# Layer 1's last group of a four-layer graph network: row sums ended pair by pair, and the gate of three pairs written in one row on TensorE

## The chip, the cores and the metric

The kernel runs on one core of one Trainium2 chip, in float32 throughout. The metric is the device time of one execution in microseconds (us); the median of several runs counts. One execution was also taken by the hardware profiler; all times inside the kernel are from it and are counted from the start of its span.

## The reference

There are N = 2708 rows of D = 256 values and one dense matrix `adj` (2708 x 2708). Four layers follow one another; each has a graph part and a feed-forward part, and both are added to x. The change lies in layer 1:

```python
# graph part
A = adj + eye;  D = 1 / sqrt(sum(A, axis=1));  A = A * D[:, None] * D[None, :]
x = x + relu(A @ (layernorm(x) @ W) + b)
# feed-forward part: one of 8 experts for each row, by its gate
H      = gelu(layernorm(x) @ W1 + b1)             # 256 -> 1024, the same W1 for all
probs  = softmax(H @ Wg + bg);  assign = argmax(probs)
x      = x + probs[assign] * (H @ Wd[assign] + bd[assign])
```

## The kernel before

**Tiles and groups.** The rows are cut into 22 tiles of 128 (the last has 20 rows). In layer 1 they are worked off in three groups, tiles 0 to 7, 8 to 15 and 16 to 21 (`GROUPS1`). A group's graph part is a loop over the 22 row blocks j of `adj`: SyncE loads the row block `adrow` (four buffers), VectorE makes a mask of it (L1165) and adds the identity where the block meets the group's own rows (L1168), and TensorE adds one product for each of the group's tiles (L1196) into PSUM banks `acc2` that hold two tiles each, a pair. After the last j, `grow` (L1147, L1149) adds the sums to x on VectorE. In the last group the pairs are tiles 16 and 17, tiles 18 and 19, and tile 20 with the 20 last rows (tile 21, whose sums come earlier from `last_sums`).

**The gate, `send1`.** For a group it takes mean and variance of the rows (`stats`, with an inverse root of eleven short VectorE instructions), and then goes pair by pair: normalise (L187), turn on TensorE (`turn_to`, L203), copy on ScalarE (L204), the products with W1 into eight blocks of 128 hidden values (`hidden`, L357) with Gelu on ScalarE (L359), the gate's products (L1092), a copy (L1095), their addition over four quarters (L1099, L1100). H itself is transposed on VectorE (L1109, into two buffers `hrow`) and stored in device memory as `hid`, by ScalarE's queue in the last group and by GpSimd's in the others (L1115, L1118). Then come softmax, the choice of an expert and `route` (L384, L386 on TensorE), which gives each row its place in a list ordered by expert; GpSimd scatters each row's name and weight there (`taken`, L495).

**The blocks, `Units`.** The second product goes in blocks of 128 rows of one expert. For each block GpSimd gathers the names (L509), then the rows of `hid` into one of three buffers `hs` (L649); TensorE turns them (L660, eight transposes) and ScalarE copies them into one of three buffers `hTs` (L661); SyncE loads the expert's weights `wb` of 1,152 KB (L1032, three buffers); TensorE multiplies (L699, into one of two PSUM banks `yacc`); VectorE adds the bias and multiplies by the weight (`ys`, L700, L701); GpSimd scatters the result (`given`, L495). Blocks 0 to 8 (`NA` = 9) hold rows of the first two groups only, so that they can run before the last group is routed; blocks 9 to 23 need that routing. After the last scatter layer 2 loads `given` (`mine`, L56).

**What sets the order.** Each engine works off its own list in the order in which it stands. The framework's planner makes that list from the order of the source, its own costs and the dependences; `add_manual_dep` with `NoSync` fixes the order of two instructions in it, with no semaphore. Loads, stores, gathers and scatters stand in the lists of the engines that issue them (SyncE, ScalarE, GpSimd), and a waiting one holds up those behind it. In the kernel before, blocks 0 to 8 come after `send1` in the source, and the planner mixes the two.

Of the kernel before, what the change touches and what calls it, by code (L numbers as in the profile page):

```python
# [8 lines left out]
F32 = mybir.dt.float32  # L9
# [57 lines left out]
def adj_ffn4(ctx: ExitStack, tc: tile.TileContext, a: dict, out: bass.AP):  # L67
# [79 lines left out]
    def after(i, past):  # L147

        tc.add_manual_dep(i.ins, past, mybir.DependencyInfo(
            mybir.DependencyClass.NoSync, mybir.DependencyReason.DATA), reason="order")  # L150

    def rsqrt(pool, val, n):
# [467 lines left out]
    class Units(Blocks):  # L620
# [58 lines left out]

        def run(self, pool, items, during=None):  # L680
            self.names_todo += items
            self.todo += items
            self.rows_todo += len(items)
            self.more()
            turned = self.turn(pool, self.rows[0][1])
            n = 0
            while self.rows:
                w2, hT = self.ahead.pop(0), turned
                m, _ = self.rows.pop(0)
                self.more()  # L690
                if during is not None:
                    during(n)
                n += 1
                if self.rows:
                    turned = self.turn(pool, self.rows[0][1])
                y = pool.tile([P, D], F32, name="ys", bufs=2)
                q = pools["psum"].tile([P, W], F32, name="yacc", bufs=2)[:, :D]
                for f in range(HC):
                    te.matmul(q, lhsT=hT[:, f, :], rhs=w2[:, f, :], start=(f == 0), stop=(f == HC - 1))  # L699
                v.tensor_tensor(y, q, w2[:, HC, :], ALU.add)  # L700
                v.tensor_scalar(y, y, m[:, 1:2], None, op0=ALU.mult)  # L701
                scatter(self.given, m[:, 0:1].bitcast(I32), y, self.given.shape[0] - 1, self.ok)

    def count_left(pool, *what):
# [317 lines left out]
    with ExitStack() as l1:  # L1022
# [47 lines left out]

        def send1(tiles):

            G = len(tiles)
            t0 = tiles[0]
            st = stats(tiles)
            names = gt.tile([P, GM, 2], F32, name="names", bufs=1)[:, :G]
            lg = gt.tile([P, G, E], F32, name="lg", tag=f"lg{G}")
            v.memset(lg[:, G - 1, :], 0.0)
            for i0 in range(0, G, 2):
                own = [(i, (i - i0) * P, rows(tiles[i])) for i in range(i0, min(i0 + 2, G))]  # L1080
                w = own[-1][1] + own[-1][2]
                xT = gt.tile([P, DC, 2 * P], F32, name="xT4", bufs=2)
                for i, k, r in own:
                    xn = work.tile([P, D], F32, name="xn")[:r]
                    norm_to(xn, tiles[i], i, st)
                    turn_to(xT[:, :, k : k + r], xn, r)
                hT = gt.tile([P, HC, 2 * P], F32, name="hT", bufs=1)
                hidden(hT, xT, w1, lambda f: b1[:, f : f + 1], 0, w, HC)
                p = ps_tmp()
                for f in range(HC):  # L1090
                    q = f % 4 * Q
                    te.matmul(p[q : q + Q, :w], lhsT=wg[:, f, :], rhs=hT[:, f, :w],  # L1092
                              start=(f < 4), stop=(f >= HC - 4), tile_position=(0, q))
                lT = gt.tile([P, 2 * P], F32, name="lT", bufs=1)
                s.copy(lT[:, :w], p[:, :w])  # L1095
                p = ps_tmp()
                for i, k, r in own:
                    o = p[:r, (i - i0) * E : (i - i0 + 1) * E]
                    te.matmul(o, lhsT=lT[:, k : k + r], rhs=fold[:, :E], start=True, stop=True)  # L1099
                    v.tensor_tensor(lg[:r, i, :], o, bg[:r], ALU.add)  # L1100

                queue = s if tiles is GROUPS1[-1] else g
                for i, k, r in own:
                    h = gt.tile([P, P // Q, HC * Q], F32, name="hrow", bufs=2)
                    n = -(-r // Q)
                    if r < P:
                        v.memset(hT[:, :, k + r : k + n * Q], 0.0)
                    for f in range(0, HC, 4):
                        v.transpose(h[:, :n, f * Q : (f + 4) * Q].rearrange("p b (f i) -> p f b i", i=Q),  # L1109
                                    hT[:, f : f + 4, k : k + n * Q].rearrange(  # L1110
                                        "p f (b j) -> p f b j", j=Q))
                    for q in range(P // Q):
                        dst = hid[tiles[i] * P : tiles[i] * P + r, q * HC * Q : (q + 1) * HC * Q]
                        if r == P:
                            queue.dma_start(dst.rearrange("(b j) c -> j b c", j=Q),  # L1115
                                            h[q * Q : (q + 1) * Q])
                        else:
                            queue.dma_start(dst, h[q * Q : q * Q + r, 0, :])  # L1118
            pin()
            probs = softmax8(gt, lg, G)  # L1120
            sel, best = first_max(gt, probs, G)
            g.tensor_copy(names[:, :, 0:1].bitcast(I32), choice1[:, t0 : t0 + G, :])
            v.tensor_copy(names[:, :, 1:2], best)
            ix = route(gt, (sel,), G, t0 * P, rows(tiles[-1]), known)
            for i, t in enumerate(tiles):
                r = rows(t)
                scatter(taken[1], ix[:r, i, :], names[:r, i, :], N - 1, "taken1")
# [5 lines left out]
                lambda t, r, p, by: s.activation(sup[:r, t, :], p, AF.Copy, scale=by))  # L1133
        hid = tc.dram_tile([N, HC * P], F32, name="hid")
        work1 = Units(hw, given[1], weights1, hid)
        for tiles in GROUPS1:
# [3 lines left out]
            pairs = banks(tiles)  # L1140
            acc = [gsum.tile([P, 2, D], F32, name="acc2", bufs=4) for _ in pairs]

            def grow(p, t, m, q):
# [8 lines left out]
            for j in [*range(12), FULL, *range(12, FULL)]:  # L1152
# [33 lines left out]
                if j == FULL:  # L1186
                    for n, t, k in by_turns(own):
                        last_product(acc[n // 2][:, n % 2, :], n // 2, ad, k, sup[:, FULL, :],
                                     False)
                    continue  # L1190
                for p, pair in zip(acc, pairs):
                    for n in pair:
                        if n == len(own):
                            continue
                        _, k, q = own[n]
                        te.matmul(p[:q, n - pair[0], :], lhsT=ad[:, k : k + q],  # L1196
                                  rhs=sup[:r, j, :], start=(j == 0 and n == pair[0]),
                                  stop=(j == FULL - 1 and n == pair[-1]))
            for p, pair in zip(acc, pairs):
                if pair[0] < len(own):  # L1200
                    t, m = own[pair[0]][0], len(pair)
                    grow(p[:, :m, :], t, m, P)
            if end:
                sums.close()
# [5 lines left out]
                    tc.tile_pool(name="c1", side="right", reuse_waits="tile", bufs=1))  # L1210
                work1.more()
            send1(tiles)
            if tiles is GROUPS1[-2]:
# [6 lines left out]
        more = [(rest, b, past, taken[1], False) for b in range(ALWAYS, MOST - NA)]  # L1220
        left = []

        def beside(b):
            if b == NA + 4:
                left.append(blocks_left(too_many, MOST))
                as_bc = row_bc(work, "L2_gnn_attn_src", D, "elu_e")
                ad_bc = row_bc(work, "L2_gnn_attn_dst", D, "elu_e")
                g.dma_start(w_l2[:, :, :D], a["L2_gnn_WT"].rearrange("(c p) n -> p c n", p=P))
                score_columns(w_l2, D, as_bc, 1, D)
                score_columns(w_l2, D, ad_bc, 1, D + 1)  # L1230
                centre(w_l2)

        work1.run(hc, items, beside)
        work1.run_rest(hc, more, left[0])

# [19 lines left out]

    def in_order(first, engines):

        was = {}
        for i in nc.cur_bb.bb.instructions[first:]:
            if i.engine in engines:  # L1260
                if i.engine in was:
                    tc.add_manual_dep(i, was[i.engine], mybir.DependencyInfo(
                        mybir.DependencyClass.NoSync, mybir.DependencyReason.DATA), reason="order")
                was[i.engine] = i.name


# [4 lines left out]
    with tc.tile_pool(name="t3", reuse_waits="tile", bufs=1) as t3:  # L1271
# [7 lines left out]
        psum_pool(sums, 3, 5)  # L1279
        tp = t3  # L1280
        wr = mat(tp, "L2_ffn_Wr", E)
        br = row_bc(tp, "L2_ffn_br", E)
# [7 lines left out]
        wa = tp.tile([P, DC, D + 2 * NH], F32, name="w_l3")  # L1290
        g.dma_start(wa[:, :, :D], a["L3_gnn_WT"].rearrange("(c p) n -> p c n", p=P))

        SUMMED = NT - 2
# [633 lines left out]
```

## Time and profile before

| | us |
|---|---|
| median of 3 runs (lowest, highest) | 1924.65 (1923.59, 1931.69) |
| the profiled execution, its own time | 1928.12 |
| its span | 1926.4 |
| TensorE busy | 1825.9 (95%) |
| VectorE, ScalarE, GpSimd busy | 1095.6, 641.6, 342.8 |
| mean granted TensorE clock | 0.979 |

A float32 product is two instructions in the trace, so that the eight products of a block are sixteen. Timeline rows give start, length, engine, line, operation, tiles, count, and in brackets how long the engine stood idle before and what ended that. Line numbers are those of the kernel before.

### The profile page before, as it was taken

How to read it: one execution, taken by the hardware profiler on the slowest of the kernel's cores; microseconds unless marked ns; L12 is line 12 of the kernel's file. 1: busy time of each engine (PE TensorE's matmuls, PEld its weight loads, DVE VectorE, ACT ScalarE, POOL GpSimd, SP SyncE). 2: the span in 40 equal slices, each digit the busy share in tenths (PEclk: the TensorE clock that was granted, in tenths of full speed). 3: DMA queues.
4: the chain of work that ended last, by engine and by line, in shares of the span. 5: the costliest groups of instructions: out<-in, count | busy, mean ns of one | idle time of the engine just before them, and what ended most of it. 6: DMA issues, size and time to landing. Idle time of an engine off the chain costs nothing.

```text
span 1926.4 us, 25726 instructions
## 1 busy us (share of the span) xinstructions
PE 1825.9 (95%) x9453; PEld 1326.4 (69%) x9453; DVE 1095.6 (57%) x2483; ACT 641.6 (33%) x1457; POOL 342.8 (18%) x405
## 2 busy tenths in 40 slices
PE   7999999999998999999787799999899999999998
PEld 6888788888887888887676678888556732232344
DVE  7777872443434443354432265555354398999897
ACT  7868752222223204021222142222242552031131
POOL 1004254333321002213436300000000000000000
PEclk9999999999998999999898899999899999999999
DMA  8435658887764454636777610000101000001000
GB/s 275 138 111 163 215 200 296 317 317 287 269 265 139 125 156 116 152 109 130 227 231 283 252 54 1 1 1 1 44 1 34 17 1 23 23 12 28 20 20 15
DMA packets 90141, 243.94 MB, mean 127 GB/s; under 512 B 18159, under 2 KB 44823, under 8 KB 80792
## 3 DMA queue, kind: packets, MB, share of 16 engines
q1 hardware_dynamic: 70048, 197.09, 31.1%
q0 software_dynamic: 16960, 42.42, 7.0%
q10 hardware_dynamic: 3000, 2.70, 0.5%
q8 instruction: 78, 1.28, 0.3%
q14 instruction: 55, 0.45, 0.1%
HBM read 216.29 MB, written 28.71 MB: 127 GB/s over the span
## 4 chain that ended last, share of the span: by engine, by line
PE 71%; DMA 14%; DVE 6%; issue 4%; ACT 2%; POOL 2%; SPq 0%; POOLq 0%; DVEq 0%; ACTq 0%
PE num L1825 10%; PE ps_acc L1404 9%; PE acc L907 9%; PE acc L1196 8%; PE ps_tmp L357 7%; DMA given<-ys,xs 6%; PE den L1835 5%; PE ps_acc L573 4%; PE ps_tmp L250 4%; PE yacc L607 4%; PE ps_acc L1588 3%; DMA hs<-hid,names 2%; DMA names<-taken,b_ix 1%; DVE e L1795 1%; DMA given<-ys,names 1%
## 5 line engine op out<-in xcount | busy, mean ns | idle before, releaser
L1795 DVE SCALAR_TENSOR_TENSOR e<-arena,G,mask 128x1024 f32<-128x1024 f32 (+1 forms) x264 | 287.0, 1150 | 13.6 <-PE den L1835 13.6
L1825 PE MATMUL num<-e,wh 128*64 128x512 f32 (+4 forms) x1056 | 215.5, 551 | 0.0
L907 PE MATMUL acc<-msg,wt 128*128 128x256 f32 x882 | 200.1, 384 | 1.9 <-DVE x L932 1.9
L1404 PE MATMUL ps_acc<-hh,e 128*128 128x257 f32 x882 | 199.2, 382 | 1.7 <-ACT o L1349 1.7
L1196 PE MATMUL acc<-sup,adrow 128*128 128x256 f32 x882 | 198.6, 381 | 1.5 <-DVE adrow L1168 1.5
L907 PEld LDWEIGHTS acc<-msg,wt 128*128 128x128 f32 x882 | 166.9, 192 | 28.1 <-DVE x L932 2.6
L1196 PEld LDWEIGHTS acc<-sup,adrow 128*128 128x128 f32 x882 | 165.0, 190 | 28.5 <-issue 5.2
L1404 PEld LDWEIGHTS ps_acc<-hh,e 128*128 128x128 f32 x882 | 163.7, 190 | 29.2 <-ACT o L1349 4.3
L573 PE MATMUL ps_acc<-xTs,wa 128*128 128x256 f32 (+1 forms) x768 | 169.4, 373 | 3.0 <-DVE xTs L563 2.9
L607 PE MATMUL yacc<-wb,hTs 128*128 128x256 f32 x736 | 168.3, 380 | 0.0
L575 ACT ACTIVATE hTs<-ps_acc,wa 128x256 f32<-128x256 f32 (+1 forms) x192 | 88.9, 465 | 235.4 <-PE yacc L607 161.2
L573 PEld LDWEIGHTS ps_acc<-xTs,wa 128*128 128x128 f32 x768 | 136.5, 190 | 29.4 <-DVE xTs L563 5.8
L1825 PEld LDWEIGHTS num<-e,wh 128*64 128x64 f32 (+1 forms) x1056 | 66.6, 136 | 126.9 <-issue 106.2
L607 PEld LDWEIGHTS yacc<-wb,hTs 128*128 128x128 f32 x736 | 137.1, 190 | 17.7 <-DVE ys L609 0.2
L1398 DVE SCALAR_TENSOR_TENSOR e<-Rb,G,mask 128x640 f32<-128x640 f32 (+2 forms) x110 | 85.1, 775 | 93.1 <-PE ps_acc L1404 93.0
L1835 PE MATMUL den<-e,wh 128*32 128x512 f32 (+4 forms) x1056 | 118.0, 548 | 0.0
L204 ACT COPY xT<-ps_tmp 128x256 f32<-128x256 f32 x98 | 33.7, 365 | 243.2 <-PE ps_tmp L203 219.5
L1165 DVE TENSOR_SCALAR mask<-adrow 128x1024 uint8<-128x1024 f32 (+1 forms) x66 | 41.7, 631 | 123.4 <-DMA adrow<-in_adjT 123.2
L699 PE MATMUL yacc<-wb,hTs 128*128 128x256 f32 x384 | 91.2, 389 | 0.0
L865 DVE SCALAR_TENSOR_TENSOR wt<-adrow,wt 128x640 f32<-128x640 f32 (+3 forms) x67 | 71.1, 1064 | 28.9 <-ACT wt L141 28.5
L1835 PEld LDWEIGHTS den<-e,wh 128*32 128x32 f32 (+1 forms) x1056 | 30.2, 108 | 77.8 <-issue 73.7
L495 POOL DMA_INDIRECT given<-ys,xs x46 | 65.5, 1424 | 81.0 <-DVE ys L610 68.0
(454 smaller groups left out, 2572.7 us busy)
## 6 DMA issues: line engine op xcount, KB each, us to landing
adhalf<-in_adjT SPq DMA_DIRECT2D x42, 677.0 KB
wb<-in_L_ffn_W2p SPq DMA_DIRECT2D x24, 1152.0 KB
wb<-in_L_ffn_Wdp SPq DMA_DIRECT2D x24, 1152.0 KB
wa<-in_L_ffn_W1b SPq DMA_DIRECT2D x24, 1028.0 KB
adrow<-in_adjT SPq DMA_DIRECT2D x42, 512.0 KB
adrow<-in_adjT SPq DMA_DIRECT2D x42, 320.0 KB
adrow<-in_adjT SPq DMA_DIRECT2D x21, 576.0 KB
adrow<-in_adjT SPq DMA_DIRECT2D x21, 448.0 KB
```

The source lines that it names most:

```text
L357: te.matmul(p[:, :w], lhsT=w1[:, c, f * P : (f + 1) * P], rhs=xnT[:, c, c0 : c0 + w], start=(c == 0), stop=(c == DC - 1))
L573: i = te.matmul(p[:, f % 2, : m * P], lhsT=w1[:, c, f * P : (f + 1) * P], rhs=xT[:, c, : m * P], start=(c == 0), stop=(c == DC - 1))
L575: s.activation(hT[:, f, : m * P], p[:, f % 2, : m * P], AF.Gelu, bias=bias[:, f : f + 1])
L607: te.matmul(q[:, k, :], lhsT=hT[:, f, k * P : (k + 1) * P], rhs=w2[:, f, :], start=(f == 0), stop=(f == HC - 1))
L699: te.matmul(q, lhsT=hT[:, f, :], rhs=w2[:, f, :], start=(f == 0), stop=(f == HC - 1))
L907: te.matmul(p[:q, n - pair[0], :], lhsT=wt[:, k : k + q], rhs=msg[:r, j, :], start=(j == 0 and n == pair[0]), stop=(j == FULL - 1 and n == ...
L1196: te.matmul(p[:q, n - pair[0], :], lhsT=ad[:, k : k + q], rhs=sup[:r, j, :], start=(j == 0 and n == pair[0]), stop=(j == FULL - 1 and n == ...
L1398: v.scalar_tensor_tensor(e[:r, :w], Rb[:r, c0 : c0 + w], G[:r, j, :], mask[:r, j, c0 : c0 + w], op0=ALU.max, op1=ALU.mult)
L1404: te.matmul(p[:, : D + 1], lhsT=e[:, k : k + q], rhs=hh[:, j, :], start=(j == 0), stop=False)
L1795: v.scalar_tensor_tensor(e[:, :w], slow[:, m % 2, k, :w], G[:, j, 2 * pair + k, :], mask[:, j, c0 : c0 + w], op0=ALU.max, op1=ALU.mult)
L1825: te.matmul(num[k * DK : (k + 1) * DK, hf, :q], lhsT=wh[some, j, 2 * pair + k, :DK], rhs=e[some, h0 - c0 : h0 - c0 + q], start=(j == 0), s ...
L1835: te.matmul(den[z : z + Q, :q], lhsT=wh[some, i, 2 * pair + k, DK : DK + 1] .to_broadcast([some.stop - some.start, Q]), rhs=e[some, h0 - c ...
```

## The change

1. **Sums.** In the last group the products of row blocks 18, 19 and 20 are held back until all three are there, and then done pair by pair; `grow`, `stats` and the normalising of a pair follow that pair's sums (before: `stats` once for all six tiles).
2. **Gate.** `hidden` is done in halves of four blocks with three half buffers `hT` (in all groups). In the last group the order on TensorE is written out (`in_order`): first half of a pair, gate products of the pair before, second half, addition of the pair before, turning of the next pair. The block worker becomes a generator (`pieces`): the turns of blocks 0 and 1 stand around the last pair's gate products, and blocks 0 and 1 and the turn of block 2 ahead of `route`; all other blocks come later.
3. **Stores.** The last group's rows of `hid` go out on SyncE's queue, those of the last pair behind the weights of block 2.
4. **Elsewhere.** The preparation of layer 2's matrix (`beside`, for block 13) is tied behind block 12's result, and the constants of the next stage, which GpSimd loads, are tied behind the scatter of block 17 (`at_end`).

```diff
@@ Units
-        def run(self, pool, items, during=None):
+        def pieces(self, pool, during=None):
+            turned = [self.turn(pool, self.rows[0][1])]
+            yield
             n = 0
             while self.rows:
-                w2, hT = self.ahead.pop(0), turned
+                if len(self.rows) > 1:
+                    turned.append(self.turn(pool, self.rows[1][1]))
+                    yield
+                w2, hT = self.ahead.pop(0), turned.pop(0)
...
                 scatter(self.given, m[:, 0:1].bitcast(I32), y, self.given.shape[0] - 1, self.ok)
+                yield
@@ send1
+            else:
+                v.memset(lg[:, G - 1, :], 0.0)
+                start = len(nc.cur_bb.bb.instructions)
+                was, xT = None, turned(pairs[0])
+                for n, own in enumerate(pairs):
+                    hTs = [half(own, xT, 0)]
+                    if was is not None:
+                        lT = gate_products(*was)
+                    hTs.append(half(own, xT, 1))
+                    if was is not None:
+                        add_up(was[0], lT)
+                        keep(*was, nc.sync)
+                    if n + 1 < len(pairs):
+                        xT = turned(pairs[n + 1])
+                    was = own, hTs
+                next(fill)
+                lT = gate_products(*was)
+                next(fill)
+                add_up(own, lT)
             pin()
             probs = softmax8(gt, lg, G)
...
+            if ready is not None:
+                for _ in range(3):
+                    next(fill)
             ix = route(gt, (sel,), G, t0 * P, rows(tiles[-1]), known)
+            if ready is not None:
+                in_order(start, (mybir.EngineType.PE,))
+                keep(*was, nc.sync)
@@ the loop over row blocks
+                kept_rows.append((j, ad))
+                if end and FULL - 4 < j < FULL - 1:
+                    continue
                 for p, pair in zip(acc, pairs):
-                    for n in pair:
...
+                    for jj, ad in kept_rows:
+                        for n in pair:
...
+                kept_rows.clear()
+            ready = []
+            for n, (p, pair) in enumerate(zip(acc, pairs)):
                 if pair[0] < len(own):
                     t, m = own[pair[0]][0], len(pair)
                     grow(p[:, :m, :], t, m, P)
+                    if end:
+                        two = tiles[2 * n : 2 * n + 2]
+                        st = stats(two)
+                        ready += [normed(two, i, st) for i in range(2)]
...
+                between = work1.pieces(hc, lambda b: beside(b))
+                send1(tiles, ready, between)
+                break
@@ the next stage
+        for i in nc.cur_bb.bb.instructions[begin:]:
+            if i.engine == mybir.EngineType.Pool:
+                tc.add_manual_dep(i, work1.at_end, mybir.DependencyInfo(
+                    mybir.DependencyClass.NoSync, mybir.DependencyReason.DATA), reason="order")
```

## The prediction

> **What bounds the kernel now.** I read the page's busy shares first (TensorE 95%: any gain lies in its gaps), then the busy time by stretches around the change, then TensorE's timeline, VectorE's waits and GpSimd's timeline. The stretches (us of each engine, instructions in brackets, then clock, DMA share, GB/s):
>
> ```profile
> core 0: us, PE busy (x) PEld busy (x) DVE busy (x) ACT busy (x) POOL busy (x), PEclk, DMA share, GB/s
> 900.00:921.00 21.00, 19.52 (x91) 16.85 (x90) 8.27 (x26) 0.00 (x0) 11.52 (x12) 1.00 0.69 110
> 921.00:943.00 22.00, 10.53 (x46) 8.68 (x45) 9.60 (x42) 3.42 (x6) 10.91 (x10) 0.69 0.82 290
> 943.00:983.00 40.00, 40.00 (x251) 33.01 (x250) 12.64 (x32) 17.75 (x40) 8.90 (x10) 1.00 0.77 239
> 983.00:1005.00 22.00, 20.19 (x112) 17.55 (x110) 12.85 (x58) 4.64 (x8) 9.95 (x11) 1.00 0.70 202
> 1005.00:1021.00 16.00, 0.08 (x1) 0.00 (x0) 2.13 (x7) 0.00 (x0) 10.59 (x13) 0.61 0.85 236
> 1021.00:1042.00 21.00, 20.33 (x105) 17.91 (x106) 4.50 (x13) 5.47 (x10) 14.13 (x14) 0.89 0.67 218
> 1042.00:1081.00 39.00, 36.44 (x202) 31.52 (x201) 6.96 (x18) 8.92 (x17) 22.41 (x22) 1.00 0.99 382
> ```
>
> Two gaps of TensorE can be filled: 11.5 us of 921 to 943, most of the rest there at a low clock, and all 16 us of 1005 to 1021. The last stretch is another limit: DMA is 99% busy. TensorE's timeline and VectorE's waits say why:
>
> ```profile
> 924.36 1.09 PE L660 MATMUL ps_acc<-ident,hs 128*128 128x128 f32 x8 [2.87 <-DMA hs<-hid,names]
> 931.95 1.94 PE L660 MATMUL ps_acc<-ident,hs 128*128 128x128 f32 x8 [6.50 <-DMA hs<-hid,names]
> 943.49 0.81 PE L203 MATMUL ps_tmp<-ident,xn 128*128 128x128 f32 x4
> 991.57 0.43 PE L384 MATMUL ps_tmp<-r_m,before 128*128 128x56 f32 x2 [1.81 <-DVE r_m L379]
> 1021.67 1.94 PE L660 MATMUL ps_acc<-ident,hs 128*128 128x128 f32 x8 [16.59 <-DMA hs<-hid,names]
> ```
> ```profile
> DVE ys L700 <- PE yacc L699: 22.9, 6, 12.2
> DVE hrow L1109 <- ACT hT L359: 12.0, 4, 4.6
> ```
>
> The sums end at 921.4, yet the gate's first turn stands at 943.49: the inverse root was done at 930.5, but the normalising stood on VectorE behind block 0's `ys`, which waited 12.2 us for its product. So the gate ended at 983, `route` at 993.3, and the names of blocks 9 on were due only after this on GpSimd:
>
> ```profile
> 995.24 0.98 POOL L495 DMA_INDIRECT taken<-names,r_ix  x1 [4.65 <-issue]
> ...
> 1001.72 0.92 POOL L495 DMA_INDIRECT taken<-names,r_ix  x1 [0.30 <-issue]
> ...
> 1010.26 1.04 POOL L509 DMA_INDIRECT names<-taken,b_ix  x1 [0.30 <-issue]
> ...
> 1014.80 1.07 POOL L649 DMA_INDIRECT hs<-hid,names  x1 [0.30 <-issue]
> ```
>
> Block 8 ended at 1004.1 and block 9 could start only at 1021.67. From there 15 blocks took 70.6 us, to 1092.25, the point that I move; the last scatter and the load behind it (to 1099) stay as they are.
>
> **Sums.** Row blocks 18 to 20 are ready at 914.2, 916.5 and 917.7 (VectorE's rows). Products cost 0.216 us an instruction (16 in 3.46). Pair 0 waits for each row block and ends at 918.7 (before: 920.1); pairs 1 and 2 need 12 and 6 instructions more: 922.6, that is 1.2 us later.
>
> **To the first turn.** From 918.7 VectorE's new order has four `grow` (1.6 us), two statistics (1.0), then pair 0's inverse root mixed with the `grow` and statistics of the other pairs, some 29 instructions. Long and short ones together took 0.40 us a couple at 926 to 929, so 5.6 us: first normalised tile at 927.0, turn at 927.1 instead of 943.5. Two more inverse roots are 22 short instructions; they lie in this mix or beside TensorE.
>
> **Clock.** TensorE would stand idle from 922.6 to 927.1, 4.5 us. The rows above show eight transposes in 1.09 us after 2.87 us of idleness and 1.94 us after 6.50; 4.5 lies between, so the price is 0 to 2.2 us (the start at 1021.67: transposes +0.9, six products 2.63 instead of 1.30). I take 2, nearer to the cold row. The Trainium skill, TensorE: Matmul & The Clock Gate, section Part 1: The HAM clock gate, speaks against the change here: half clock after about 3.4 us without work, full clock after about 3.4 us of work, by which this gap would cost 1.7.
>
> **The gate in a row.** Pair 0: turn, copy and 32 instructions, the first six cold: to 936.9. Pair 1: turn 0.64, wait for ScalarE's copies (est. 0.85: a Gelu of 0.47 and two copies of 0.37 less overlap), two halves of 3.46, pair 0's gate products 1.19 and addition 0.28: 946.8. Pair 2 with 148 columns: 0.6 + 0.6 + 2.0 + 1.2 + 2.0 + 0.3: 953.5. Two block turns of 0.87, gate products 0.9 and an addition (0.6 with its copy): 957. Blocks 0 and 1 and a turn: 7.8, to 964.8, which covers softmax (2.3 us of VectorE from 989.22 to 991.52, a table load of 1.28 and `ys` 0.8; uncovered it would cost some 5). `route` 1.73: **966.5** instead of 993.3.
>
> **Stores.** ScalarE spent 12.4 us issuing 24 of them (3.88 for eight), gone from the Gelus' engine. On SyncE they stand ahead of block 2's weights, needed at 967 and issued by some 955. VectorE's second pair of `hrow` waits for the first pair's stores; before that was 3.6 us at most, and here the gap is about 6, so nothing, or 3.6 if uncovered.
>
> **The new wait.** On TensorE the turns of blocks 5, 6, 7 and half of 8 now stand ahead of block 4's products. On GpSimd the gather of block 6 stands ahead of the six scatters of `taken`, that of block 7 behind them, and that of block 8 behind block 9's names, which wait until the scatters have landed. At 1.30 us an entry, counted from `route`'s end: gather 6 at 1.0 to 2.1 (it waits for turn 3), scatters to 9.8, names 8, gather 7 to 12.4, one scatter, then names 9. Scatters land 2.2 to 12.2 us after issue (median 4.5); the last before issued until 1002.64 and released GpSimd by 1008.9, so I take 6.0: names 9 at 15.8, a scatter, gather 8 to 19.4. Gathers land 3.3 to 13.2 us later (median 7.7); the one at 1014.80 needed 5.7, in a lull like this (three weight buffers full), so 5.0. TensorE has only 10.4 us of work there (turns 3 to 6, blocks 2 and 3), and block 4 starts at 25: **991.5**, after 13 us of idleness in two pieces. The Trainium skill, DMA: Bandwidth & Descriptors, section Anatomy of one DMA — SWDGE (gpsimd) path, gives 2.0 us plus bytes / 436e3 for such a transfer, which would be 2.0 and 3.2 us and bring block 4 forward by 5.8; no gather here was that quick.
>
> **To the end.** Blocks 4 to 7 (13.8), half a turn (0.4) and the cold clock (2): 1007.8 for block 9's turn, before 1021.67. From there 70.6 as before, less 2.2 for the cold start that stood there; DMA keeps its 4.70 us a block (nine turns from 1041.98 to 1084.31). Added: the `centre` products of 1.03, before in the gap, with 0.3 of waiting for VectorE. The constants stand behind gather 22: five loads of 3.2 us, a scatter, gather 23, two loads more; `w_l3` lands 6.6 us later, 12 us after block 18, and eight VectorE instructions (3.0) on it stand between `ys` 19 and 20. So `ys` 20 comes 6 us late; block 22 waits for its bank (1.5) and block 23 for its weights (0.7): 2.2, between 0 and 5. Sum 71.9: the end at **1079.7** against 1092.25, 12.5 us gained. The other two groups get half buffers too; TensorE was idle 6.5 of 300 us there, so 0 to 1, taken as 0. Instructions behind this stage stand as before.
>
> The profiled execution, 1928.12, would become 1915.6; it lies 3.5 above the median, so I forecast 1924.65 - 12.5 = **1912**.
>
> **Rivals.** *Quick landings:* both at their shortest rows (2.2 and 3.3, not 6.0 and 5.0) give 5.5 us, a clock that stays up 2 more: a gain of 18 to 20, 1905. For it: little DMA traffic at 970 to 990. Against: the medians. *The end is DMA's:* from 1042 to 1081 it was 99% busy, and a sooner TensorE meets fuller queues; if the last 15 blocks took 4.9 us each (+5) and the constants cost 5, the gain is 4.7: 1920, no change by my bound. *Late landings, the other side:* scatter and gather at their longest rows, 12.2 and 13.2, put block 4 14.4 us later, and the kernel 1.9 us slower, 1926.5; it decides from a sum of 23.5 us on, against the 11 taken, and every further late gather adds. *That the order isn't kept* can be excluded: it stands so in TensorE's list.
>
> **Numbers.** Forecast 0.5 (1908 to 1917), quick 0.2, DMA's end 0.2, late 0.1. The range leaves out half of the late case and the outer edge of the quick one: 1903 to 1922. A run can tell about 0.5%, 9.6 us, from no change. Faster by more: the quick case and four fifths of the forecast's, 0.2 + 0.42 = 0.62. Slower by more: 0.07, the late case with repeated delays. The same: 0.31.
>
> **What would show it.** Right: first gate turn near 927, `route` ending near 966, then TensorE idle before the turns of blocks 7 and 8 with `hs` named as releaser, no gap before block 9, last product near 1080. Wrong: a gate that waits on VectorE or ScalarE past 960; block 4 after 1000; blocks 9 to 23 well above 72 us, with DMA or `w_l` named; or no idleness between 975 and 992.

## The result and the profile after

The changed kernel took 1928.78 us (median of 12 runs, 1924.14 to 1935.88), the kernel before 1926.14 beside it: ratio 1.0009, 95% interval 0.999 to 1.0028. That is no change, where 1912 was forecast; 1928.78 lies outside the forecast range. The profiled execution took 1928.52, its span is 1926.8.

The line numbers of the changed kernel are new: L203 became L213, L386 L396, L495 L505, L509 L519, L649 L659, L660 L670, L699 L719, L700 L720. The stretches of the changed kernel, cut at the same times as those of before:

```profile
core 0: us, PE busy (x) PEld busy (x) DVE busy (x) ACT busy (x) POOL busy (x), PEclk, DMA share, GB/s
...
921.00:943.00 22.00, 16.84 (x83) 13.16 (x82) 12.32 (x65) 8.53 (x18) 3.14 (x4) 0.92 0.86 287
943.00:983.00 40.00, 33.94 (x229) 29.48 (x227) 17.98 (x72) 14.65 (x31) 17.16 (x17) 0.95 0.71 214
983.00:1005.00 22.00, 13.16 (x51) 11.12 (x51) 1.55 (x4) 2.25 (x4) 10.11 (x10) 0.63 0.52 156
1005.00:1021.00 16.00, 16.00 (x89) 14.23 (x88) 3.11 (x8) 3.13 (x6) 10.27 (x10) 1.00 0.96 346
...
1042.00:1081.00 39.00, 34.24 (x182) 28.54 (x181) 4.68 (x12) 7.52 (x14) 23.35 (x26) 1.00 0.93 344
1081.00:1093.00 12.00, 9.34 (x36) 7.51 (x37) 4.89 (x14) 2.46 (x3) 2.96 (x3) 0.72 0.36 123
```

The gaps that the change aims at are filled: 921 to 943 went from 10.53 to 16.84 us of TensorE, 1005 to 1021 from 0.08 to 16.00. But 983 to 1005 fell from 20.19 to 13.16 at a clock of 0.63, and DMA rested there too (0.70 to 0.52 of its time). TensorE's timeline shows the same by place:

```profile
926.63 0.67 PE L213 MATMUL ps_tmp<-ident,xn 128*128 128x128 f32 x4 [4.02 <-DVE xn L197]
927.77 8.80 PE L367 MATMUL ps_tmp<-xT,L_ffn_W 128*128 128x256 f32 x32 [0.48 <-ACT xT L214]
...
965.06 1.46 PE L396 MATMUL ps_tmp<-r_m,all_ones 128*128 128x48 f32 x12
...
981.07 1.94 PE L670 MATMUL ps_acc<-ident,hs 128*128 128x128 f32 x8 [4.96 <-DMA hs<-hid,names]
987.20 1.94 PE L670 MATMUL ps_acc<-ident,hs 128*128 128x128 f32 x8 [4.19 <-DMA hs<-hid,names]
993.79 1.08 PE L670 MATMUL ps_acc<-ident,hs 128*128 128x128 f32 x4 [4.65 <-DMA hs<-hid,names]
994.67 9.40 PE L719 MATMUL yacc<-wb,hTs 128*128 128x256 f32 x32
...
1011.25 1.04 PE L670 MATMUL ps_acc<-ident,hs 128*128 128x128 f32 x8
...
1080.97 1.66 PE L670 MATMUL ps_acc<-ident,hs 128*128 128x128 f32 x8 [2.38 <-DMA hs<-hid,names]
1085.05 5.22 PE L719 MATMUL yacc<-wb,hTs 128*128 128x256 f32 x16 [2.43 <-DVE ys L720]
1090.50 3.69 PE L719 MATMUL yacc<-wb,hTs 128*128 128x256 f32 x16 [0.23 <-DMA wb<-in_L_ffn_Wdp]
```

The gate starts at 926.6 instead of 943.5 and `route` ends at 966.5, both within half a microsecond of the forecast. Then three waits for rows, 13.8 us in all, stand ahead of block 4; block 9's turn comes at 1011.25, 10.4 us sooner than before; and the last product ends at 1094.2, 1.9 us later than before. The whole lead is lost between these two points. From here on the **stage** is the time from the end of the group's sums to the end of block 23's product: 170.8 us before (921.5 to 1092.25), 171.6 after (922.6 to 1094.2). It is read from one execution of each kernel; medians scatter by some 3 us against it, so differences of 2 or 3 us between two stages are not to be read as effects. TensorE's waits inside the stage, by what ended them (us in total, times, longest us), first of the kernel before:

```profile
PE ps_acc L660 <- DMA hs<-hid,names: 30.6, 8, 16.6
PE ps_tmp L384 <- DVE r_m L379: 1.8, 1, 1.8
```

and of the changed one:

```profile
PE ps_acc L670 <- DMA hs<-hid,names: 20.0, 11, 5.0
PE ps_tmp L213 <- DVE xn L197: 4.0, 1, 4.0
PE yacc L719 <- DVE ys L720: 2.4, 1, 2.4
PE ps_tmp L367 <- ACT xT L214: 1.5, 3, 0.7
```

The change took 10.6 us of waiting for rows away, but other waits rose from 1.8 to 8.9 us, and TensorE's busy time in the stage from 138.3 to 142.6 us with as many instructions: the 32 products that took 8.80 and 9.40 us above need 6.9 when warm. The question is what holds the rows.

### The profile page after: what moved, and what is told of

It reads as the page before. It is cut to its first block, busy times and chain, and to the rows that moved or that the text cites. A ratio compares the mean times of both kernels' runs of the same rounds, so it can differ in the third digit from the quotient of the medians.

```text
span 1926.8 us, 25763 instructions
## 1 busy us (share of the span) xinstructions
PE 1829.5 (95%) x9453; PEld 1327.0 (69%) x9453; DVE 1096.7 (57%) x2510; ACT 642.8 (33%) x1457; POOL 341.8 (18%) x405
## 5 line engine op out<-in xcount | busy, mean ns | idle before, releaser
L1290 PEld LDWEIGHTS acc<-sup,adrow 128*128 128x128 f32 x882 | 165.0, 190 | 28.2 <-issue 5.5
L617 PEld LDWEIGHTS yacc<-wb,hTs 128*128 128x128 f32 x736 | 137.1, 190 | 17.9 <-DVE ys L619 0.6
L719 PE MATMUL yacc<-wb,hTs 128*128 128x256 f32 x384 | 90.9, 392 | 2.7 <-DVE ys L720 2.4
L887 DVE SCALAR_TENSOR_TENSOR wt<-adrow,wt 128x640 f32<-128x640 f32 (+3 forms) x67 | 71.1, 1064 | 27.7 <-ACT wt L141 27.3
L719 PEld LDWEIGHTS yacc<-wb,hTs 128*128 128x128 f32 x384 | 74.0, 198 | 13.4 <-DVE ys L720 2.8
```

What stands on the lines that cost most here:

```text
L617: te.matmul(q[:, k, :], lhsT=hT[:, f, k * P : (k + 1) * P], rhs=w2[:, f, :], start=(f == 0), stop=(f == HC - 1))
L1290: te.matmul(p[:q, n - pair[0], :], lhsT=ad[:, k : k + q], rhs=sup[:, jj, :], start=(jj == 0 and n == pair[0]), stop=(jj == FULL - 1 and n ...
```

## The experiments

**Theories.** *The two waits:* the turns of blocks 5 to 8, which stand ahead of block 4's products in TensorE's list, and the constants on GpSimd ahead of the last gathers, ate the gain. *The transfers:* the blocks run at the pace of their transfers, so that a stage which starts sooner only waits for them later. A third, tested once, was *a loop of latencies* (names, then rows).

The kernels of one group (1 to 4, 5 to 8, 9 to 11, 12 to 14) ran on one chip with the kernel before beside them, whose median there was 1925.45, 1939.37, 1940.34 and 1940.22 us. From run 5 on the group's sums end at 933 to 937 instead of 921 to 926, with the kernel before (runs 5 and 13) as with the changed one; so ratios and stages are compared, not times.

| run | edit of the changed kernel | us | ratio to before | stage, us |
|---|---|---|---|---|
| - | before, in the first comparison | 1926.14 | 1 | 170.8 |
| - | the change | 1928.78 | 1.0009 (0.999 to 1.0028) | 171.6 |
| 1 | constants free | 1924.91 | 0.9997 (0.9987 to 1.0007) | 172.2 |
| 2 | written order to block 8 | 1917.24 | 0.996 (0.9946 to 0.9975) | 162.3 |
| 3 | five row buffers | 1923.04 | 0.9988 (0.9976 to 1.0) | 160.9 |
| 4 | half weights | 1906.68 | 0.9913 (0.9896 to 0.993) | 151.0 |
| 5 | half weights, on the kernel before | 1932.31 | 0.9941 (0.9919 to 0.9963) | 162.2 |
| 6 | 1 and 2 | 1935.7 | 0.9977 (0.9961 to 0.9994) | 163.0 |
| 7 | names further ahead | 1938.96 | 0.9985 (0.9972 to 0.9998) | 170.6 |
| 8 | 1, 2 and 3 | 1935.66 | 0.9975 (0.9962 to 0.9987) | 162.0 |
| 9 | fourth weight buffer | 1931.9 | 0.996 (0.9948 to 0.9972) | 159.8 |
| 10 | 9 and 2 | 1927.04 | 0.9927 (0.9913 to 0.9941) | 156.2 |
| 11 | half weights and 2 | 1920.76 | 0.9891 (0.9876 to 0.9906) | 152.0 |
| 12 | a third of the weights | 1924.07 | 0.9917 (0.9896 to 0.9938) | 153.7 |
| 13 | the same, on the kernel before | 1928.76 | 0.9942 (0.992 to 0.9965) | 157.0 |
| 14 | a third of the weights and 2 | 1921.43 | 0.9905 (0.9884 to 0.9926) | 154.7 |

Behind `route` the planner makes TensorE's list, and an edit can move its choice. By the timelines block 4's products stand where the change left them, behind half of block 8's turn, in runs 1 and 3, up to a turn earlier in runs 4 and 7, and right behind block 5's turn in runs 2, 6, 8, 10, 11 and 14, where the order was written, but also in runs 9 and 12, where it was not. Runs 9 and 12 so hold a second change.

**1. Constants free.** The tie of GpSimd's six loads to block 17's scatter is taken out:

```diff
-        for i in nc.cur_bb.bb.instructions[begin:]:
-            if i.engine == mybir.EngineType.Pool:
-                tc.add_manual_dep(i, work1.at_end, ...)
```

> The changed kernel without the tie of the next stage's constants behind block 17's scatter; GpSimd then issues them between the gathers of blocks 10 and 11, where it stood idle for 4.5 us. Theory A (two waits ate the gain: the turns ahead of block 4's products, and the constants at the end): the three pauses of TensorE behind block 20 (2.4, 2.4 and the cold clock) go, the last block's product ends near 1087 instead of 1094, and the kernel is 6 to 8 us faster than the changed one, some 1921. Theory B (the transfers of this stage set its end, so that time saved ahead of them returns as slower blocks): the end moves by 2 us at most.

The stage is 172.2 us; the 6 to 8 us of the two waits' theory (A) did not come. The wait for `ys` at the end is gone, but TensorE now waits for weights in the middle (`wb`, four times, 1.8 us at most) and for rows near the end (2.8, 1.1 and 1.5 us). The constants cost nothing that the transfers do not take anyway.

**2. Written order to block 8.** The written order on TensorE takes in all of blocks 0 to 8, so that each block's products stand right behind the next block's turn:

```diff
-                in_order(start, (mybir.EngineType.PE,))
+                written.append(start)
...
-        for _ in between:
-            pass
+        for k, _ in enumerate(between):
+            if k == 13:
+                in_order(written[0], (mybir.EngineType.PE,))
```

> The changed kernel with TensorE's written order continued to block 8: the products of blocks 4, 5 and 6 stand behind the turns of blocks 5, 6 and 7, no longer behind those up to 8. Theory A: blocks 4 and 5 fill 7 of the 14 us of idleness at 976 to 994, block 9's turn comes near 1004 to 1006 instead of 1011, the kernel is 4 to 7 us faster. Theory B: the gap is smaller, but the blocks behind it wait longer for transfers, and the end moves by 2 us at most.

A gain of 9.3 us in the stage and 0.5% by the ratios, more than either theory gave it (4 to 7 us, at most 2). Its waits for rows fell from 20.0 to 8.8 us. The order matters, then; but is that its own price, or what it lets the transfers do? Counted from the end of the sums, 17.8 MB had moved after 82 us in the changed kernel and 21.3 MB here (DMA rates of the stretches, added up): with block 4's product done sooner (54.4 us after the sums instead of 72.1) a weight buffer comes free sooner, and the engines rest less. 3.5 MB are 10 us at the 347 GB/s shown below.

**3. Five row buffers.** Two halves of W1's tile, idle after the gate, take rows too:

```diff
-            h = self.hs[self.places[1] % 3]
+            h = self.hs[self.places[1] % len(self.hs)]
...
+                work1.hs += [w1[:, 0, :], w1[:, 1, :]]
+                work1.more()
```

> The changed kernel with five buffers for gathered rows instead of three: the two new ones lie in the gate's weights W1, which are free once the last pair's products are done. The gathers of blocks 3 to 7 then stand ahead of the scatters of names on GpSimd. Theory A: at most 3 us of idleness before block 4, block 9's turn near 1000, the kernel 8 to 14 us faster than the changed one (constants as in the change). Theory B: 3 us at most, with TensorE waiting for weights or rows behind block 9 instead.

Block 4 came 56.0 us after the sums instead of 72.1, and the stage kept 10.7 of these 16 us: then VectorE waited up to 14.7 us for the scatter that held `ys`, and TensorE 8.0 for VectorE. The time kept only 4 us of it (ratios 0.9988 and 1.0009), between the theories' guesses: from the last product to the span's end it took 836.5 us instead of 832.6, and the sums ended 3 us later.

**4. Half weights.** 640 KB a block: the second half of the weights is left out and the first used twice, so that the product is a wrong one, with as many instructions:

```diff
-                    te.matmul(q, lhsT=hT[:, f, :], rhs=w2[:, f, :], ...)
-                v.tensor_tensor(y, q, w2[:, HC, :], ALU.add)
+                    te.matmul(q, lhsT=hT[:, f, :], rhs=w2[:, f % 4, :], ...)
+                v.tensor_tensor(y, q, w2[:, 4, :], ALU.add)
...
-            wb = wbs["pool"].tile([P, 2048 + D], F32, name="wb", bufs=3)
+            wb = wbs["pool"].tile([P, 1024 + D], F32, name="wb", bufs=3)
```

> The changed kernel with only the first half of each expert's weights loaded in layer 1 (640 KB a block instead of 1,152), used for both halves of the product: part of the computation is left out, and the instructions on TensorE are the same. Theory A: 24 blocks move 13 MB less, gathers land somewhat sooner, the kernel is 3 to 6 us faster, and the waits before block 4 and behind block 20 stay. Theory B: blocks 9 to 23 run at TensorE's 4.33 us without a wait, and the kernel is 10 us or more faster.

The clearest answer: 20.6 us off the stage, with no wait of TensorE touched by hand, as the transfers' theory (10 or more) and not the other (3 to 6) had it. Block 4's products came 8.3 us sooner (63.8 us after the sums), and the other 12.3 us were won behind them. These are the stretches from turn 9 to turn 22 of the changed kernel (13 blocks), and of turns 8 to 23 with half weights:

```profile
1011.25:1074.06 62.81, 58.95 (x317) 50.18 (x316) 13.71 (x36) 13.96 (x26) 39.02 (x41) 1.00 0.96 347
```
```profile
996.86:1062.70 65.84, 65.84 (x365) 58.68 (x364) 15.58 (x42) 16.11 (x30) 44.55 (x47) 1.00 0.81 272
```

With full weights 62.81 us at 347 GB/s are 21.8 MB, 1.68 MB a block (weights, rows, results); at TensorE's 4.33 us a block that would need 387 GB/s, and the engines, busy 96%, give 347 (381 in the last stretch of the kernel before, so the margin is small). With half weights they are busy 81% and TensorE has not a gap in 65.84 us.

**5. Half weights on the kernel before.** The same edit there.

> The kernel before with 640 KB of weights a block in layer 1 instead of 1,152 KB (each block's second product reads the first four weight tiles twice, so the product itself is left wrong; its instructions stay as many and as long). It is the counterpart of the earlier run in which the changed kernel with half weights took 1906.7. Theory of the transfers (the block phase runs at the transfers' pace whenever it starts, so that what is won ahead of it is lost in it): with the weights halved both kernels run their blocks at TensorE's 4.33 us, so the kernel before gains little, because its 15 turns after turn 9 took 62.6 us of 15 x 4.33 = 65 already: about 1921 (1917 to 1925), and the changed kernel is then 10 to 18 us faster than it. Theory of the two waits (written order and constants cost the change its gain, whatever the transfers do): the kernel before gains as much from the halving as the changed one, some 20 us, to 1905 to 1908, and the difference stays near nothing.

The stage is 162.2 us, 11.2 longer than that of run 4; but by the ratios the two are only 0.28% apart, 5.4 us. The kernel before gained 11 us by the ratio and 8.6 by the stage, between the theories' guesses (up to 9, and some 20); the difference of 10 to 18 us that the transfers' theory foretold is met by the stage alone. Runs 12 to 14 ask again on one chip.

**6. Runs 1 and 2 together.**

> Both waits of the theory of the two waits are taken away: TensorE's written order holds to block 8 (as in the run at 1917.2) and GpSimd's six loads of the next stage's constants no longer have to stand behind the last gather. Theory of the two waits: the constants cost 5 to 8 us in that run as well (turn 23 waited 2.4 us for its rows, its product 2.8 us for the sum of block 21), so 1909 to 1912. Theory of the transfers: the loads are transfers wherever they stand; beside the blocks they push gathers and weights back as in the run with the constants alone free (1924.9, 3.9 us under the changed kernel), so 1914 to 1918.

163.0 us, as run 2 alone; the ratio, 0.9977 against run 2's 0.996 on another chip, shows no gain either, and is short of both theories' ranges. The constants are out of it.

**7. Names further ahead.**

```diff
-            while self.names_todo and len(self.named) + len(self.rows) < 4:
+            while self.names_todo and len(self.named) + len(self.rows) < 8:
```

> The changed kernel with up to 8 instead of 4 blocks' names and rows together fetched ahead. Theory of a loop of latencies (a block's names landing in 7.3 us and then its rows landing in 8.5 us, with three blocks' rows under way, are what set 4.8 to 5.0 us a block): names are there long before, the loop holds the rows alone, 8.5 / 3 = 2.8 us a block, and the blocks fall to TensorE's 4.33: 1920 to 1924. Theory of the transfers: the names are 5 KB a block, nothing moves: 1927 to 1930. Theory of the two waits: nothing moves either, since neither wait is on names except 2.6 us at the first names after the route: 1926 to 1929.

170.6 us of stage, as without it. The ratio, 0.9985, lies where the loop's theory had put it, so the two readings differ by some 4 us. In the trace turns 9 to 22 took 58.9 us instead of 62.8, but the gate's first turn came 2.4 us later after the sums, a wait of 7.6 us for rows stood behind block 4's products and ahead of block 5's, and at the end TensorE waited 1.7 and 3.0 us: what names further ahead can win is small, and it was not won in the stage. The loop is not excluded as a part of a block's time.

**8. Runs 1, 2 and 3 together.**

> All three edits at once: five buffers for rows instead of three (two are halves of a weight tile that is idle), written order to block 8, constants free. Theory of the two waits: with both waits gone and the rows of blocks 7 and 8 gathered before the route's scatters, block 4 starts near 981 and the last product ends near 981 + 20 x 4.33 + 1 = 1069, 25 us before the changed kernel's: 1900 to 1908. Theory of the transfers: five buffers only queue more gathers behind the same weights, as in the run with the five buffers alone (13 us won at block 4, 7.5 left at the last product): 1911 to 1918.

Both waits are gone and the stage is 162.0 us, as with run 2's or run 3's edit alone; TensorE waits for weights instead, 5.9 us in five pieces. The ratio, 0.9975, misses both theories' ranges. Four ways of taking away most of the wait ahead of block 4 (runs 2, 3, 6, 8) all end between 160.9 and 163.0, and what is left there is not set by TensorE's order.

**9. Fourth weight buffer.** W1's tile and 1 KB beside it take every fourth block's weights:

```diff
+            wbs["n"] = wbs.get("n", -1) + 1
+            if wbs["n"] % 4 == 3:
+                bias = wbs["pool"].tile([P, 1, D], F32, name="wbias", bufs=1)
+                ...
+                nc.sync.dma_start(w1.rearrange("p c n -> p (c n)"), src[:, :2048])
...
-            while weights and self.todo and len(self.ahead) < 2:
+            while weights and self.todo and len(self.ahead) < self.deep:
```

> The changed kernel with a fourth place for a block's weights: W1's tile (8 KB a partition, idle once the last gate is done) and 1 KB beside it take every fourth block's weights, from block 3 on, so SyncE can be three blocks ahead instead of two. All bytes are loaded as before, some of them earlier. Measured from the end of the group's sums to the last product of block 23 (171.6 us in the changed kernel, 170.8 before). Theory of the transfers: what counts is how many bytes have moved when TensorE starts on block 4; the 16 DMA engines were 52% busy from 983 to 1005 with three full weight buffers, and one more block of 1,152 KB is 3.4 us at the 344 GB/s of the stretches after 1005: 167 to 169, a time 3 to 4 us under the changed kernel's. Theory of the two waits: block 4 waits for its turn in the written order, not for weights: 171 to 172, no gain.

159.8 us: 11.8 off the stage, and more than the theory's 3 to 4. But the buffer is not alone in it: TensorE's list is another one too, with block 4's products right behind block 5's turn, 53.7 us after the sums, as in run 2. Its timeline there (the products are L721 in this run; W1's tile, `L_ffn_W`, holds block 3's weights, so the `wb` that follows is block 4's), and its waits for rows:

```profile
982.33 3.62 PE L721 MATMUL yacc<-L_ffn_W,hTs 128*128 128x256 f32 x16
985.78 1.04 PE L671 MATMUL ps_acc<-ident,hs 128*128 128x128 f32 x8
986.65 2.54 PE L721 MATMUL yacc<-wb,hTs 128*128 128x256 f32 x11
```
```profile
PE ps_acc L671 <- DMA hs<-hid,names: 10.6, 5, 8.8
```

The 8.8 us stand ahead of block 8's turn, and of block 5's products behind it; only 1.8 us are left elsewhere, against 6.2 behind block 4 in the changed kernel. 2.5 MB more than in the changed kernel had moved 82 us after the sums, 7 us at 347 GB/s. How much of the 11.8 is the buffer's, run 9 can't say; run 10 beside run 2 can.

**10. Fourth weight buffer, written order to block 8.**

> The same fourth weight buffer, with TensorE's written order to block 8 (alone: 162.3 us from the end of the sums to the last product, ratio 0.996). Theory of the transfers: 3 to 4 us less again, 158 to 160, ratio 0.994. Theory of the two waits: nothing more to gain by weights, 162, ratio 0.996.

156.2 us of stage and a ratio of 0.9927: this version beats both kernels, by 13 us against the one before. With TensorE's order the same as in run 2, the fourth buffer is worth 6.1 us of stage, 0.33% by the ratios (on two chips), more than the 3 to 4 of the transfers' theory and against the nothing of the other. Some of it may be lost behind the stage: the runs that reuse W1's tile (3, 8, 9, 10) take 833.8 to 836.5 us from there to the end, the others 830.4 to 832.9.

**11. Half weights, written order to block 8.**

> The changed kernel with both edits, 640 KB of weights a block (the second product reads four weight tiles twice, so its result is left wrong) and the written order to block 8: what the written order costs when the transfers are out of the way. With half weights alone the stage from the end of the sums to the last product took 151.0 us, with one wait of 7.9 us for rows ahead of block 4 and one of 1.0 us near the end. Theory of the two waits: the order's price is those waits, 7 to 9 us whatever the weights: 142 to 144, ratio about 0.987. Theory of the transfers: the 9.3 us that the order was worth with full weights were weights loaded sooner; with half weights most of it is gone: 147 to 151, ratio 0.989 to 0.991.

152.0 us: no shorter than the 151.0 without the order, and by the ratios 0.0022 apart, inside the intervals. The 9.3 us of full weights are not there. Of what run 4 waited for, the 7.9 us for rows went; 4.0 us for a copy of ScalarE and 2.2 for VectorE at layer 2's matrix came, and `ys` took 1.7 instead of 1.0.

**12, 13, 14. A third of the weights** (384 KB a block) on the changed kernel, on the kernel before, and with the written order to block 8, on one chip.

> The changed kernel with 384 KB of weights a block instead of 1,152 KB (the second product reads two weight tiles four times, so its result is left wrong; instructions as many and as long). Both theories: TensorE at 4.33 us a block from block 4 on. Theory of the transfers: with less traffic the scatters and gathers around the route land sooner still, so the stage from the end of the sums to the last product is at or under the 151.0 of half weights: 146 to 151, ratio to the kernel before 0.988 to 0.991. Theory of the two waits: the waits for the rows of blocks 6 to 8 stay as long as in the changed kernel, 13.8 us: 154 to 157.

> The kernel before with the same 384 KB a block. Theory of the transfers: its TensorE gaps before the gate and behind the route stay, since neither waits for weights, and the stage is about the 162 of half weights, 159 to 163; the changed kernel with the same weights is 10 to 14 us shorter, about the 12.5 that were forecast. Theory of the two waits: the change is worth nothing with any weights: within 3 us of the changed kernel with the same weights.

> The changed kernel with 384 KB a block and the written order to block 8. Theory of the transfers: with full weights the order was worth 9.3 us because the weights were loaded sooner; here that is worth nothing, and what is left is TensorE's idleness ahead of block 4, at most the 7 us seen with half weights: 0 to 5 us under the run without the order, on the same chip. Theory of the two waits: the whole wait goes, 7 to 9 us under it.

The stages are 153.7, 157.0 and 154.7. Run 14 is no second test of the order, since run 12 has block 4's products behind block 5's turn already (56.6 us after the sums, 54.8 in run 14); that the order has hardly a price of its own rests on run 11 beside run 4, two chips. Run 12 is no faster than the half weights' 151.0, as the transfers' theory had it (146 to 151), and just under the other's 154 to 157. Two more guesses of the transfers' theory fell: the kernel before dropped to 157.0, not 159 to 163, and the change is worth 3.3 us by the stage and 0.25%, 4.8 us, by the ratios, not 10 to 14. That is near the "within 3 us" of the two waits' theory, whose reason, 13.8 us of waits for rows, is not in the trace. TensorE's waits, first of run 13, then of run 12:

```profile
PE ps_acc L660 <- DMA hs<-hid,names: 14.6, 3, 10.6
PE ps_tmp L384 <- DVE r_m L379: 1.8, 1, 1.8
```
```profile
PE ps_tmp L213 <- DVE xn L197: 5.2, 1, 5.2
PE ps_tmp L245 <- DVE w_l L270: 3.1, 1, 3.1
PE yacc L719 <- issue: 2.5, 4, 1.0
PE ps_tmp L367 <- ACT xT L214: 1.5, 3, 0.7
```

With light transfers the kernel before waits 14.6 us for rows instead of 30.6, so half of these waits, which the change set out to fill, was the transfers' time from the start. Run 12 has none of the 14.6, but 5.2 us ahead of the gate, 3.1 at layer 2's matrix and some 6 of small waits.

## Why the prediction was wrong, by its own steps

| step | forecast | measured |
|---|---|---|
| sums end | 922.6 | 922.6 |
| first turn of the gate | 927.1 | 926.6 |
| clock, price | 2 (0 to 2.2) | 2.0 |
| gate ends, `route` ends | 957, 966.5 | 957.1, 966.5 |
| idle ahead of block 4 | 13 in two pieces | 13.8 in three |
| block 4's products | 991.5 | 994.67 |
| block 9's turn | 1007.8 | 1011.25 |
| from there to the end | 71.9 | 82.9 |
| last product | 1079.7 | 1094.2 |

**Up to `route`: right.** Every step held within 0.5 us, the clock among them: the first 32 products took 8.80 us where warm ones take 6.9 (two of 3.46), at a granted clock of 0.63 from 926.6 to 930.6, 0.90 to 933.0 and 1.00 behind, and turn and products together cost 2.0. The Trainium skill, TensorE: Matmul & The Clock Gate (Part 1: The HAM clock gate), agrees here: the estimate worked out from it was 1.7.

**The new wait: right in kind, 3.2 us short.** Its idleness was read correctly from the lists. The landings were not the ones taken:

```profile
976.52 0.92 POOL L505 DMA_INDIRECT taken<-names,r_ix  x1 [0.30 <-issue]
...
981.70 1.00 POOL L659 DMA_INDIRECT hs<-hid,names  x1 [2.90 <-DMA hs<-hid,names]
...
986.62 1.02 POOL L519 DMA_INDIRECT names<-taken,b_ix  x1 [2.59 <-DMA taken<-names,r_ix]
```

The last scatter was issued by 977.4 and let names 9 go at 986.6: 9.2 us, where I took 6.0 out of 2.2 to 12.2. That alone is 3.2 us. The gather of block 6 landed 11.4 us after its issue, which made the third piece, and that of block 8 3.5, where I took 5.0. By the formula of the Trainium skill, DMA: Bandwidth & Descriptors (Anatomy of one DMA — SWDGE (gpsimd) path), an estimate of 2.0 us for the scatter and 3.2 for a gather, only the quickest of them comes near; the measurement decides. "A lull" was the wrong reason for a short landing: between 975 and 990 a block's weights of 1,152 KB were on their way beside them.

**"To the end 70.6 as before": the step that failed**, 11.0 us, in three parts. *3.5 us are an error of counting:* in the kernel before, block 8's products were done before block 9's turn, in the changed one its turn stands ahead of them, so 16 products remained and not 15. *1.9 us* are slower blocks between turns 9 and 22. *5.6 us* are the end: turn 22 to the last product took 20.1 us instead of 12.3, where I had given the constants 2.2. Runs 1 and 6 show that the constants were not the cause: without them the same time was lost to weights and rows.

Behind the last two is the assumption that a block's time goes with the block, wherever the transfers stand when it starts. It goes in good part with the bytes that are still to come. All kernels with full weights move 44 to 46 MB in the stage; of these had moved (DMA rates of the stretches, added up):

| | MB after 82 us | MB after 100 us | stage, us |
|---|---|---|---|
| before | 19.8 | 24.4 | 170.8 |
| the change | 17.8 | 24.0 | 171.6 |
| run 2 | 21.3 | 27.3 | 162.3 |
| run 9 | 20.2 | 26.8 | 159.8 |
| run 10 | 21.5 | 28.2 | 156.2 |
| run 3 | 19.7 | 24.3 | 160.9 |

With its gate 17 us sooner the changed kernel had moved 2 MB less than the one before when it had 82 us behind it: while TensorE stood ahead of block 4 the weight buffers stayed full, and the DMA engines rested. So what I priced as 13 us of TensorE's idleness was paid once more, as transfers not made. Bytes are not all of it: run 3 had moved no more than the two kernels, and yet ended 10 us sooner, with TensorE further ahead and 399 GB/s in the next 20 us; why it got that rate is open. I saw the engines busy 99% in the kernel before and made a rival of it (*the end is DMA's*, 0.2, 1920: no change, as it came out), but priced it as slower blocks at the end and the constants only. The transfers also hold much of the very gaps that I counted as gain: with a third of the weights the kernel before loses 16.0 of its 30.6 us of waits for rows.

**What stays open.** How much the change would be worth with no transfers in the way: 3.3 and 11.2 us by the stages of the two pairs (12 and 13; 4 and 5, on two chips), 4.8 and 5.4 by their ratios, whose intervals overlap; in run 12 TensorE's order is not that of the change. It is under the forecast 12.5 either way. The row sums and the queue of the stores were not tried alone, since the steps they belong to came out as forecast.

## What to carry to other kernels

When a stretch shows the DMA engines 96 to 99% busy, work out the bytes of a block and the rate that the compute's pace would need (387 GB/s here, against 347 given, and 381 at best over 42 us of the kernel before); where they don't give it, time won on the compute engines ahead of it is in large part paid back as waits for data, and what counts is above all how many bytes have moved by then. So look for DMA engines that rest (0.52 of 983 to 1005) and give them something to load: an order that frees a buffer sooner (9.3 us of stage) and a further buffer on top of it (6.1) did what 17 us of an earlier gate did not. When an edit is meant to change one thing, look in the timeline whether the planner has kept the rest: in runs 9 and 12 it had not. And when instructions are moved past a mark that a sum starts from, count again what remains behind the mark.

## What the runs showed of the hardware

After 4.0 us without work products ran slow, but the very first instructions not always: after 4.02 to 4.25 us the first four transposes took 0.66 or 0.67 us in some runs (the changed kernel, 3, 4, 9) and 1.09 in others (1, 10, 11, 14), against 0.60 to 0.64 warm, and the 32 products behind them 8.6 to 9.2 us in all of these, against 6.9.

Nearly the same busy share of the 16 DMA engines moved quite different amounts in this mix of long loads and gathered rows: 347 GB/s at 96% over 62.8 us in the changed kernel, 381 at 99% over 42.3 us in the one before. A busy share of 0.96 to 0.99 did not say here how much they carry.
